# Query and key projections in 2x2 blocks of seven half-deep products, with the queries' rms division moved into the masking step

## The chip, the cores and the metric

The kernel runs on one core of a Trainium2 chip. [...] The metric is the device time of one execution in microseconds; lower is better. The kernel before took 1167.87 us (median of three runs, 1166.95 to 1168.11).

## The reference

Input x is 32 sequences of 32 tokens with 512 features, fp32 throughout. Four layers are added to it in turn:

```
x = x + mix(x)        # a 32x32 matrix per sequence, picked from 16
x = x + base(x) + lora(x)   # 512x512, and a rank-32 part picked from 5
x = x + adapt(x)      # a 512x512 matrix per sequence, picked from 8
x = x + attention(x)
```

The attention layer is the one that changes:

```
q = x @ Wq.T   # 32 heads of 128;  k, v = x @ Wk.T, x @ Wv.T: 8 heads of 128
q, k = rmsnorm(q) * q_norm_w, rmsnorm(k) * k_norm_w     # over the 128 of a head
q, k = rope(q, pos), rope(k, pos)                       # halves of a head turned by cos, sin
k_all, v_all = 512 rows of a paged cache (16 pages of 32), then the 32 new rows
scores = q . k_all / sqrt(128), masked where the cached row is past the sequence's length
out = softmax(scores) @ v_all, heads joined, @ Wo.T
```

Four query heads share one key head. There are 1024 tokens, so 8 tiles of 128.

## The kernel before, in words

**Stage 1** (0 to about 123 us) does the first three layers for the eight tiles t, software-pipelined, and turns each finished tile into `x3t(t)`: 512 features as 4 slices (KC) of 128 on the partitions, 128 tokens in the columns. The `adapt` matrices, 1 MB each and 32 of them, stream in on SyncE.

**The query and key stage** (123 to 401 us). The weights of q, k and v are 12 chunks (NCH) of 512 outputs, that is 4 heads: chunks 0 to 7 queries, 8 and 9 keys, 10 and 11 values. A chunk's weights are loaded by `load_qkv` (L303, 1 MB). For each chunk and tile `project` (L322) makes four matmuls (`project_part`, L307, L308) of 128x512, summed in one PSUM bank. Then, for queries and keys: `squares` on ScalarE (L335, from PSUM), `sums` on VectorE (L339), `roots` (L343), `inverses` (L347), `rotate`, `scales` (L366, one ScalarE multiplication per head) and `store_heads`. `rotate` forms product times cosine table (L351) and two halves of product times sine table (L356) on VectorE, straight from the PSUM bank, and adds them on GpSimd (L362). The norm weights lie in the tables `cw` and `sw`. `store_heads` transposes 32x32 blocks on VectorE (L375) and stores four transfers to DRAM (`q_d`, `k_d`; L384). `projected_evenly` (L402) writes out by hand the order of these steps on TensorE, VectorE and ScalarE, one tile behind; GpSimd and SyncE are not in that hand order. Values (chunks 10, 11) are only copied (L315) and stored to `v_d`. Chunk 0 and one tile of chunk 1 are done within stage 1. In this stage the pages of keys and values of the first two sequences are loaded (`load_pages`, `load_values`, the latter as indirect transfers on GpSimd, L246), and 20 of the 32 heads' output weights (`load_wo(0, ...)`, 16 transfers of 320 KB on SyncE, L692).

**Attention** (from 401 us) runs over 256 units (sequence b, key head g), written out by hand for all five engines. A unit n does: scores (two matmuls, L754, L755, into one pair of PSUM banks that all units share), then on VectorE the masking step L763: scores times -1/sqrt(128) plus the mask, with its minimum `low`; on ScalarE the exponential with its sum (L772); transposes and placements (L785, L797 ScalarE, L799 GpSimd, L801 VectorE); eight units later the products with the values (L825). The rest of TensorE's time carries the output projection (`share` and `finish`, L902) from unit 37 on, and in units 0 to 36 `fill`: one matmul of chunk 11 (values) at a time, 32 of them with five units left empty. Pages for sequence b+1 are loaded on SyncE in the first half of sequence b, 12 at its first unit and 4 at its fifth. The other 12 heads' output weights (`load_wo(1, ...)`, 192 KB each) follow from unit 37 on.

Two places of stage 1 matter for the prediction too: `angles` makes the tables, whose products run on GpSimd (L577 to L580), and `mixers` multiplies two SBUF tiles of 128x128 on VectorE (L463, then L470 adds the identity).

Of the kernel before, what the change touches and what calls it, by code (L numbers as in the profile page):

```python
# [12 lines left out]
F32 = mybir.dt.float32  # L13
# [7 lines left out]
P = 128  # L21
# [14 lines left out]
HALF = HQ // 2  # L36
QUAD = 4
AHEAD = 8
VS_BUFS = 4
# [18 lines left out]
def cond_resid_kernel(  # L58
# [29 lines left out]
    x_d = dram.tile([NT, P, HID], F32, name="x_d")  # L88

# [30 lines left out]
    eps_t = const.tile([P, 1], F32, name="eps_t")  # L120
    half_pi = const.tile([P, 1], F32, name="half_pi")
# [8 lines left out]
    def constant_values():  # L130
# [3 lines left out]
        nc.gpsimd.memset(eps_t, EPS)  # L134
        nc.gpsimd.memset(half_pi, HALF_PI)
# [63 lines left out]
    homes, kts, vts, vns, qts = {}, {}, {}, {}, {}  # L199
# [12 lines left out]
    def see_keys(b: int):  # L212

        nc.vector.tensor_scalar(
            mask, key_i, len_f[:, b : b + 1], -1.0e30, ALU.is_ge, ALU.mult
        )
# [4 lines left out]
    def load_queries(b: int, q: int):  # L221
# [4 lines left out]
        )  # L226

# [41 lines left out]
    ahead = pa.enter_context(ExitStack())  # L269
    wqps[0] = ahead.enter_context(tc.tile_pool(name="a_wq0", bufs=1))  # L270
    turn = ahead.enter_context(ExitStack())
    wp = turn.enter_context(tc.tile_pool(name="a_w", bufs=1))
    tp = turn.enter_context(tc.tile_pool(name="a_t", bufs=3))
# [38 lines left out]
    def store_values(ps, c: int, t: int):  # L312
        c0 = (c - (HQ + HK) // REP) * HID
        vs = vsp.tile([P, HID], F32, tag="vs", name=f"vs_{c}_{t}")
        copied = nc.scalar.copy(vs, ps)  # L315
        if (c, t) == (NCH - 2, 1):

            with tc.issue_after(copied.ins):
                nc.scalar.activation(warm, eps_t, AF.Exp)
        nc.scalar.dma_start(out=v_d[t * P : (t + 1) * P, c0 : c0 + HID], in_=vs)  # L320

    def project(c: int, t: int):  # L322
        ps = accumulator(f"qkv_{c}_{t}", c >= (HQ + HK) // REP)
        for k in range(KC):
            project_part(ps, c, t, k)
        if c >= (HQ + HK) // REP:
            store_values(ps, c, t)
            return None
        return SimpleNamespace(
            c=c, t=t, i=0 if c < HQ // REP else 1, ps=ps.rearrange("p (h d) -> p h d", h=REP)  # L330
        )

    def squares(u):
        u.sq = tp.tile([P, REP, D], F32, tag="sq", name=f"sq_{u.c}_{u.t}", bufs=2)
        nc.scalar.activation(u.sq, u.ps, AF.Square)  # L335

    def sums(u):
        u.ss = tp.tile([P, REP], F32, tag="ss", name=f"ss_{u.c}_{u.t}")
        nc.vector.tensor_reduce(u.ss, u.sq, AX.X, ALU.add)  # L339

    def roots(u):
        u.rms = tp.tile([P, REP], F32, tag="rms", name=f"rms_{u.c}_{u.t}")
        nc.scalar.activation(u.rms, u.ss, AF.Sqrt, bias=eps_t, scale=1.0 / D)  # L343

    def inverses(u):
# [760 lines left out]
```

## Time and profile before

| | us |
|---|---|
| median of three runs | 1167.87 |
| the profiled execution's own time | 1172.85 |
| its span, first to last instruction | 1170.8 |
| TensorE busy | 1157.2 |
| VectorE busy | 798.3 |
| ScalarE busy | 753.4 |
| GpSimd busy | 432.0 |
| query and key stage, TensorE's unbroken run of L308 | 278.1 (123.0 to 401.1) |

"Busy" of an engine is the time in which one of its instructions ran; TensorE's matmuls overlap, so the mean time of one (593 ns) is longer than its share of the busy time. A group's line gives the source line, engine, operation, output and inputs with their shapes, the count, the busy time and the mean of one in ns, and behind the last bar the idle time of that engine just before them with what ended it. An fp32 matmul is recorded as two passes, so a count of matmuls is twice that of the program. A window's line gives each engine's busy time in a stretch of time, the granted TensorE clock (1.00 is full), the share of the transfer engines' time and GB/s. A timeline's line has the start, the time, and the instruction; "x2" means that two followed each other and are merged.

### The profile page before, as it was taken

The page shows a single profiled execution, that of the slowest core. Times are in us where ns is not written, and L with a number is a line of the kernel's source. Part 1 is how long each engine was busy: PE and PEld are TensorE (multiplying, and loading weights), DVE is VectorE, ACT ScalarE, POOL GpSimd, SP SyncE. Part 2 cuts the span into 40 slices and gives each one's busy share as a digit, 9 for nine tenths or more (in the row PEclk, how much of TensorE's full clock was granted, in tenths as well). Part 3 has the DMA queues.
Part 4 walks back from the last instruction along what each step waited for, and adds up shares of the span by engine and source line. Part 5 has one row for each costly group of instructions (what it writes and reads, how often), then busy time and mean ns, then how long its engine had stood idle before and what let it go on. Part 6 is the DMA issues. An engine that isn't in the chain of part 4 may idle for free.

```text
span 1170.8 us, 19718 instructions
## 1 busy us (share of the span) xinstructions
PE 1157.2 (99%) x5512; PEld 747.1 (64%) x5512; DVE 798.3 (68%) x1782; ACT 753.4 (64%) x1652; POOL 432.0 (37%) x571
## 2 busy tenths in 40 slices
PE   8999999999999999999999999999999999999998
PEld 5444444444444467776777777777777777777766
DVE  2524488777777168767777777777777877877861
ACT  1223376656565378877777777877877877777750
POOL 3301544333333055344433443443444344344410
PEclk9999999999999999999999999999999999999999
DMA  8997866565545647789676677767766766775710
GB/s 320 388 390 289 325 152 161 156 159 153 139 117 129 201 137 236 261 259 261 208 257 213 208 230 242 224 208 237 241 203 221 252 223 198 254 243 186 230 41 10
DMA packets 180879, 250.64 MB, mean 214 GB/s; under 512 B 21250, under 2 KB 140674, under 8 KB 175010
## 3 DMA queue, kind: packets, MB, share of 16 engines
q1 hardware_dynamic: 156802, 163.52, 45.2%
q0 software_dynamic: 19216, 69.35, 17.8%
q10 hardware_dynamic: 4752, 16.52, 4.1%
q8 instruction: 45, 0.74, 0.3%
q14 instruction: 64, 0.52, 0.1%
HBM read 219.94 MB, written 29.36 MB: 213 GB/s over the span
## 4 chain that ended last, share of the span: by engine, by line
PE 87%; DVE 4%; ACT 2%; SPq 2%; DMA 2%; issue 2%; POOL 0%; ACTq 0%; DVEq 0%; POOLq 0%
PE qkv L308 28%; PE o_ps L825 16%; PE f_ps L902 14%; PE s_ps L754 10%; PE s_ps L755 8%; PE adapt L540 2%; PE base L515 2%; DMA kt<-in_k_cache_dram 2%; ACT placed L797 1%; PE o_ps L845 1%; DVE pr L763 1%; PE pn_ps L812 1%; PE low_ps L496 1%; SPq L194 1%; ACT pr L772 1%
## 5 line engine op out<-in xcount | busy, mean ns | idle before, releaser
L797 ACT COPY placed<-turned 32x512 f32<-32x512 f32 x539 | 332.1, 616 | 32.6 <-DVE turned L785 22.9
L825 PEld LDWEIGHTS o_ps<-vt,placed 128*128 128x128 f32 x2048 | 267.9, 192 | 119.9 <-issue 95.6
L308 PE MATMUL qkv<-wq,x3t 128*128 128x512 f32 x768 | 336.7, 593 | 0.3 <-ACT vs L315 0.3
L763 DVE CUSTOM_DVE_ANT_0 pr<-s_ps,mask 128x544 f32<-128x544 f32 x256 | 185.6, 725 | 169.0 <-PE s_ps L755 153.0
L772 ACT ACTIVATE pr<-pr,low 128x544 f32<-128x544 f32 x256 | 191.6, 749 | 138.0 <-DVE low L763 93.3
L825 PE MATMUL o_ps<-vt,placed 128*128 128x128 f32 x2048 | 271.7, 276 | 2.7 <-DVE ot L882 1.3
L308 PEld LDWEIGHTS qkv<-wq,x3t 128*128 128x128 f32 x768 | 145.1, 190 | 171.4 <-issue 167.5
L799 POOL COPY placed<-turned 32x512 f32<-32x512 f32 x268 | 163.6, 610 | 228.4 <-DVE turned L785 174.6
L902 PE MATMUL f_ps<-wo,ot 128*128 128x512 f32 x480 | 242.1, 596 | 0.3
L362 POOL TENSOR_TENSOR ra<-ra,rs 128x512 f32<-128x512 f32 x80 | 101.6, 1270 | 210.5 <-DVE rs L356 189.1
L785 DVE STREAM_TRANSPOSE turned<-pr 128x512 f32<-128x512 f32 x256 | 178.6, 698 | 0.1
L754 PE MATMUL s_ps<-kt,qt 128*128 128x288 f32 x512 | 174.0, 421 | 0.6 <-issue 0.5
L755 PE MATMUL s_ps<-kt,qt 128*128 128x256 f32 x512 | 152.5, 379 | 2.0 <-DMA kt<-in_k_cache_dram 2.0
L246 POOL DMA_INDIRECT vt<-in_v_cache_dram,v_idx x128 | 127.3, 995 | 36.0 <-issue 25.0
L366 ACT ACTIVATE ra<-ra,rinv 128x128 f32<-128x128 f32 x320 | 101.8, 390 | 29.0 <-POOL ra L362 17.3
L755 PEld LDWEIGHTS s_ps<-kt,qt 128*128 128x128 f32 x512 | 97.1, 190 | 29.4 <-issue 2.8
L902 PEld LDWEIGHTS f_ps<-wo,ot 128*128 128x128 f32 x480 | 85.9, 191 | 28.2 <-issue 13.9
L801 DVE COPY placed<-turned 32x512 f32<-32x512 f32 x217 | 96.7, 445 | 5.5
L808 POOL COPY pq<-pr 128x128 f32<-128x128 f32 x64 | 18.5, 289 | 184.8 <-ACT pr L772 164.2
L754 PEld LDWEIGHTS s_ps<-kt,qt 128*128 128x128 f32 x512 | 77.5, 191 | 13.3 <-DVE low L763 5.9
L351 DVE TENSOR_TENSOR ra<-qkv,cw 128x512 f32<-128x512 f32 x80 | 54.9, 687 | 35.5 <-ACT sq L335 35.5
L335 ACT ACTIVATE sq<-qkv 128x512 f32<-128x512 f32 x80 | 47.3, 591 | 46.5 <-PE qkv L308 44.8
(99 smaller groups left out, 749.4 us busy)
## 6 DMA issues: line engine op xcount, KB each, us to landing
kt<-in_k_cache_dram SPq DMA_DIRECT2D x512, 128.0 KB
wa<-in_w_adapt_dram SPq DMA_DIRECT2D x32, 1024.0 KB
q_d<-st SPq DMA_DIRECT2D x256, 64.0 KB
qt<-q_d SPq DMA_DIRECT2D x64, 256.0 KB
wq<-in_w_qkv_dram ACTq DMA_DIRECT2D x10, 1024.0 KB
wo<-in_w_o_dram SPq DMA_DIRECT2D x16, 320.0 KB
k_d<-st SPq DMA_DIRECT2D x64, 64.0 KB
v_d<-vs ACTq DMA_DIRECT2D x16, 256.0 KB
```

The lines of the kernel that those rows point to most:

```text
L246: nc.gpsimd.indirect_dma_start(out=vts[b][:, c, :], out_offset=None, in_=v_cache, in_offset=bass.IndirectOffsetOnAxis(ap=v_idx[:, at : at ...
L308: nc.tensor.matmul(ps, x3t(t)[:, k, :], ws[c][:, k, :], start=(k == 0), stop=(k == KC - 1))
L366: nc.scalar.activation(u.a[:, h, :], u.a[:, h, :], AF.Copy, scale=u.rinv[:, h : h + 1])
L754: nc.tensor.matmul(ps[:, first:L], q, kt4[:, :N_LOW, g, :], start=True, stop=True)
L755: nc.tensor.matmul(ps[:, L : first + LT], q, kt4[:, N_LOW:, g, :], start=True, stop=True)
L763: nc.vector.tensor_tensor_reduce(pr, ps[:, first : first + LT], mask, -SCALE, 3.0e38, ALU.add, ALU.min, low)
L772: nc.scalar.activation(pr, pr, AF.Exp, bias=low, scale=-1.0, accum_out=dens[quad][:, u : u + 1])
L785: nc.vector.transpose(part, pr)
L797: nc.scalar.copy(dst, src)
L799: nc.gpsimd.tensor_copy(dst, src)
L825: nc.tensor.matmul(po, pt[:, c, :], vt[:, c, g * D : (g + 1) * D], start=(c == 0 and q == 0), stop=(c == L // P - 1 and q == 1),)
L902: nc.tensor.matmul(pfs[t][:, :HID], ots[t, h // HALF][:, h % HALF, :], wo(h), start=(h == 0), stop=(h == (HQ if t < NT - 1 else HALF) - 1),)
```

## The change: seven products for eight, and the division moved

Two neighbouring chunks (a pair) and two neighbouring tiles make a 2x2 block of outputs, and the 512 features are cut into two halves of 256. Four output tiles would take eight products of half depth (two matmuls each); the change makes seven by Strassen's scheme in Winograd's form. That needs sums of the inputs and of the results:

- `token_sums` (GpSimd, stage 1): four sums of 128x256 for each of the four pairs of tiles.
- `weight_sum` (four for each of the five pairs of chunks, 128x1024 each): on VectorE (V) or GpSimd (G), within the stage for all pairs but the first.
- `product`: two matmuls; products 6 and 7 are added onto product 1 in its bank, and 3 onto 5, after ScalarE has copied the bank out (`out_of`).
- `formed`: each output tile is the sum of a copied part and a PSUM bank (three on VectorE) or of two copied parts (one on GpSimd). It now lies in SBUF. `by_cos` (VectorE) and `by_sin` (one half on VectorE, one on GpSimd) read it there; `rotated` adds on GpSimd as before.

The queries are no longer scaled on ScalarE. Their squares are summed per head by ScalarE (`accum_out`), the inverse roots are stored to DRAM (`r_d`), loaded for each sequence, and used as the scalar per row of the masking step; the sign goes into the queries' norm weights and the mask. Keys are scaled as before.

Values of chunk 10 take chunk 0's place in stage 1; two tiles of chunk 11 are projected at the end of the stage, and the other six remain as fills in units 0 to 36. `load_wo(0, ...)` moves to attention units 1 to 16. The whole stage has a hand-written order by slots, one slot a product, GpSimd included: `at(slot, ...)` puts a step behind the product of that slot.

```diff
-VS_BUFS = 4
+VS_BUFS = 2
...
-            mask, key_i, len_f[:, b : b + 1], -1.0e30, ALU.is_ge, ALU.mult
+            mask, key_i, len_f[:, b : b + 1], 1.0e30, ALU.is_ge, ALU.mult
...
+    def load_inverses(b: int):
+        rqs[b] = const.tile([P, 2, QUAD], F32, tag="rq", name=f"rq_{b}", bufs=2)
+        nc.sync.dma_start(out=rqs[b], in_=r_d[b].rearrange("r s h g -> (r s) h g"))
...
+    PAIRS = [(HQ // REP, HQ // REP + 1)] + [(c, c + 1) for c in range(0, HQ // REP, 2)]
...
+        b11, b12, b21, b22 = w[:, 0, :KH], w[:, 1, :KH], w[:, 0, KH:], w[:, 1, KH:]
+        out, a, b = {
+            1: (d[:, 0], b12, b11),
+            2: (d[:, 1], b22, d[:, 0]),
+            3: (b12, b22, b12),
+            4: (d[:, 2], b21, d[:, 1]),
+        }[n]
+        eng.tensor_tensor(out, a, b, ALU.subtract)
...
+        nc.gpsimd.tensor_tensor(s1, b[:, :KH], b[:, KH:], ALU.add)
+        nc.gpsimd.tensor_tensor(s2, s1, a[:, :KH], ALU.subtract)
+        nc.gpsimd.tensor_tensor(s3, a[:, :KH], b[:, :KH], ALU.subtract)
+        nc.gpsimd.tensor_tensor(s4, a[:, KH:], s2, ALU.subtract)
...
+        for k in range(KH):
+            nc.tensor.matmul(
+                ps,
+                of[:, k],
+                by[:, k],
+                start=(not more and k == 0),
+                stop=(k == KH - 1),
+                skip_group_check=more,
+            )
...
+    def formed(u, a, b, eng):
+        u.x = tp.tile([P, REP, D], F32, tag="x", name=f"x_{u.c}_{u.t}", bufs=5)
+        eng.tensor_tensor(u.x.rearrange("p h d -> p (h d)"), a, b, ALU.add)
+
+    def by_cos(u):
+        u.a = tp.tile([P, REP, D], F32, tag="ra", name=f"ra_{u.c}_{u.t}", bufs=5)
         nc.vector.tensor_tensor(
-            u.a, u.ps, cw[:, u.i, u.t, :].unsqueeze(1).to_broadcast([P, REP, D]), ALU.mult
+            u.a, u.x, cw[:, u.i, u.t, :].unsqueeze(1).to_broadcast([P, REP, D]), ALU.mult
...
+        eng.tensor_tensor(
+            u.s[:, :, to],
+            u.x[:, :, of],
+            sw[:, u.i, u.t, to].unsqueeze(1).to_broadcast([P, REP, H2]),
+            ALU.mult,
+        )
...
+        for h in hs:
+            junk = tp.tile([P, D], F32, tag="sq", name=f"sq_{u.c}_{u.t}_{h}", bufs=2)
+            nc.scalar.activation(
+                junk, u.x[:, h, :], AF.Square,
+                accum_out=roots_of[half, u.t][:, h, g : g + 1],
+            )
...
+    M_ORDER = (1, 5, 2, 6, 3, 7, 4)
...
+        at(g + 1, lambda: out_of("r1", b.X, "r", 2))
+        at(g + 2, lambda: out_of("r5", b.Z, "r5", 1))
+        at(g + 3, lambda: formed(u11, b.r1, b.Y, V))
+        at(g + 3, by_cos, u11)
+        at(g + 4, lambda: out_of("r2", b.X, "r", 2))
+        at(g + 4, by_sin, u11, 0, V)
+        at(g + 4, by_sin, u11, 1, G)
+        at(g + 5, lambda: formed(u12, b.r2, b.Z, V))
+        at(g + 5, by_cos, u12)
+        at(g + 5, rotated, u11)
+        at(g + 6, lambda: out_of("r3", b.X, "r", 2))
+        at(g + 6, by_sin, u12, 0, V)
+        at(g + 6, by_sin, u12, 1, G)
+        at(g + 7, lambda: formed(u21, b.r3, b.W, V))
+        at(g + 7, by_cos, u21)
+        at(g + 7, lambda: formed(u22, b.r3, b.r5, G))
+        at(g + 8, rotated, u12)
+        at(g + 8, by_sin, u21, 0, V)
+        at(g + 8, by_cos, u22)
+        at(g + 9, by_sin, u21, 1, G)
+        at(g + 9, by_sin, u22, 0, V)
+        at(g + 9, by_sin, u22, 1, G)
+        at(g + 10, rotated, u21)
+        at(g + 11, rotated, u22)
...
+    BLOCKS = [(0, 0), (1, 0), (0, 1), (0, 2), (1, 1), (0, 3), (1, 2), (1, 3)]
+    BLOCKS += [(i, p) for i in range(2, len(PAIRS)) for p in range(NP)]
+    for n, i in ((8, 3), (12, 4)):
+        at(7 * n + 2, load_pair, i)
+    at(7 * 6 + 2, load_pair, 2)
+    for g, i in ((7 * 7, 2), (7 * 9, 3), (7 * 13, 4)):
+        at(g, weight_sum, i, 1, V)
+        at(g + 2, weight_sum, i, 2, V)
+        at(g + 4, weight_sum, i, 3, G)
+        at(g + 11, weight_sum, i, 4, G) if i > 2 else at(g + 5, weight_sum, i, 4, V)
+    at(4, weight_sum, 1, 1, V)
+    at(5, weight_sum, 1, 3, G)
+    at(6, weight_sum, 1, 2, V)
+    at(8, weight_sum, 1, 4, V)
+    at(7 * 3 + 1, load_pages, 0)
+    at(7 * 4 + 1, load_values, 0)
...
-            pr, ps[:, first : first + LT], mask, -SCALE, 3.0e38, ALU.add, ALU.min, low
+            pr,
+            ps[:, first : first + LT],
+            mask,
+            rqs[b][:, g // QUAD, u : u + 1],
...
-    fills = [(t, k) for t in range(NT) for k in range(KC)]
-    EMPTY = (10, 13, 21, 29, 34)
+    fills = [(t, k) for t in range(2, NT) for k in range(KC)]
+    FILLED = 37
...
+            if 1 <= n <= REP * REP:
+                load_wo(0, *divmod(n - 1, REP))
```

In this notation u11 and u12 are the first and second chunk of the pair at the first tile, u21 and u22 at the second; g is a block's first slot. Transposes (`store_heads`) of a query block stand at slots g+6 (u11), g+9 (u12), g+11 (u21) and g+13 (u22). For queries the squares take the place of a key block's squares, sums, roots, inverses and scales.

## Prediction

> **What bounds the kernel now.** I read the page's busy shares first, then the costliest groups, then the windows of the query and key stage, then the waits.
>
> ```profile
> span 1170.8 us, 19718 instructions
> PE 1157.2 (99%) x5512; PEld 747.1 (64%) x5512; DVE 798.3 (68%) x1782; ACT 753.4 (64%) x1652; POOL 432.0 (37%) x571
> L308 PE MATMUL qkv<-wq,x3t 128*128 128x512 f32 x768 | 336.7, 593 | 0.3 <-ACT vs L315 0.3
> L362 POOL TENSOR_TENSOR ra<-ra,rs 128x512 f32<-128x512 f32 x80 | 101.6, 1270 | 210.5 <-DVE rs L356 189.1
> ```
> ```profile
> core 0: us, PE busy (x) PEld busy (x) DVE busy (x) ACT busy (x) POOL busy (x), PEclk, DMA share, GB/s
> 160.00:200.00 40.00, 40.00 (x94) 17.67 (x93) 35.92 (x83) 28.44 (x84) 17.82 (x14) 1.00 0.62 159
> 240.00:280.00 40.00, 40.00 (x95) 17.76 (x94) 29.67 (x68) 24.09 (x70) 13.95 (x11) 1.00 0.65 178
> ```
>
> TensorE bounds this stage without a gap: 40.00 of every 40 us at clock 1.00, and 0.3 us idle before all of L308. Its chain shows 278.1 us of nothing else, from 123.0 to 401.1 us. The chain's "x8" pieces of L308 last 3.43 us, so an fp32 matmul (two recorded passes) takes 0.859 us and a tile of four 3.43 us. GpSimd has the most room (14 of 40 us).
>
> **What is removed.** Ten chunks x 8 tiles x 4 = 320 matmuls become 5 pairs x 4 x 7 products x 2 = 280. 40 x 0.859 = **34.4 us** less TensorE. A block of four tiles falls from 13.74 to 7 x 1.718 = 12.03 us. If TensorE stayed the bound, that would be all. So the question is what else fits into 12.03 us.
>
> **What is added per block.** *ScalarE* (queries): four copies out of PSUM at 0.58 (L315) and sixteen squares of 128x128 with a sum. The trace has no such square; its parts are 0.318 (L366's busy time / 320) and 0.186 for reading a sum (L772), so 0.32 to 0.576 (0.390 + 0.186) each. I take 0.50, as both rows overlap in part in the timeline: 16 x 0.50 + 2.3 = 10.3 us; even the upper end gives 11.5. It fits. Keys: four squares 0.58, roots 0.30, scales 1.28, copies: 10.9 us.
>
> *VectorE* (queries), by the pitch in the timeline (512 wide 0.60, 256 wide 0.335, transpose 0.62): three sums 1.8, four cos products 2.4, four half sin products 1.34, four transposes 2.5 = 8.0 us. Keys add four reduces and reciprocals: 4 x (0.60 + 0.14) = 2.96.
>
> *GpSimd*: five 512-wide operations at a pitch of 1.23 (L577 to L579 back to back) and four halves. A half on GpSimd is not in the trace: between 0.64 and 1.27; I take 0.69, near the lower end, since its copies of 128 and 512 columns (0.289, 0.610) leave about 0.18 fixed, (1.27 - 0.18)/2 + 0.18 less the overlap. Sum 8.9 us.
>
> Each fits alone. **But not together.** Before, the rotation on VectorE read its products from PSUM; now cos and sin products read the copied tile and the table both from SBUF, while GpSimd works from SBUF too. One place in the trace has that pair:
>
> ```profile
> 44.53 2.58 POOL L580 TENSOR_TENSOR sw<-sn,nw 128x512 f32<-128x512 f32 x2 [21.51 <-ACT sn L566]
> ```
> ```profile
> 44.80 1.16 DVE L463 TENSOR_TENSOR md<-mg,quarter 128x128 f32<-128x128 f32 x1
> 46.00 1.25 DVE L470 TENSOR_TENSOR md<-md,ident 128x128 f32<-128x128 f32 x1
> 47.18 0.68 DVE L547 TENSOR_TENSOR xs<-xs,adapt 128x512 f32<-128x512 f32 x1
> 55.17 0.28 DVE L463 TENSOR_TENSOR md<-mg,quarter 128x128 f32<-128x128 f32 x1
> ```
>
> The first column is the start, the second the time. L463 takes 0.28 us elsewhere, and 1.16 beside GpSimd's two: it ends at 45.96, 0.14 after the first GpSimd operation (44.53 + 1.29). L470 then ends 0.14 after the second. L547, with one input in PSUM, is not delayed (0.68). So a two-SBUF-input operation of VectorE waits for GpSimd's whole instruction. GpSimd lost only about 0.05 us (1.32 for 1.27), though VectorE took 0.13 in between: some 0.09 of its start lies beside it.
>
> I laid out one query block by hand with this rule, each engine in its program order, PSUM and copies ready, and 0.17 us from VectorE's end to GpSimd's start (241.81 to 241.98, L356 to L362). VectorE: form u12 to 0.60; cos u12 waits for 1.38, to 1.93; transpose u22 (of the block before) to 2.57; sin u12 waits for 3.78, to 4.07; transpose u11 4.69; form u21 5.29; cos u21 waits for 5.47, to 6.02; sin u21 6.62 to 6.91; cos u22 7.51 to 8.06; sin u22 9.24 to 9.53; transpose u12 10.15; form u11 10.75; cos u11 10.93 to 11.48; transpose u21 12.10; sin u11 12.43. GpSimd: add u11 0.15 to 1.38; sin u12 1.93 to 2.55; form u22 3.78; add u12 4.24 to 5.47; sin u21 6.02 to 6.62; sin u22 6.91 to 7.51; add u21 8.06 to 9.24; add u22 9.70 to 10.93; sin u11 11.48 to 12.08; then add u11 again at 12.60. The cycle is 12.43 us; with the one tie (2.55) given to VectorE, 12.3. I take **12.3**: just over TensorE's 12.03.
>
> [...]
>
> **Extras on the same two engines**, within the stage: weight sums (128x1024), ten on VectorE at 1.15 (from 0.414 for 256 and 0.687 for 512: 1.07 ns a column) = 11.5; six on GpSimd at 2.3 (twice 1.27 less the fixed part) = 13.8; eight gathers of values at 1.0 (L246) = 8.0, now queued between GpSimd's additions, which VectorE's transposes wait for; the keys' 2.96 x 4 = 11.8. Together 45.1. The lower bound is 0 (all beside waits of the other engine), the upper 45.1; I take three quarters, 33.8, since the hand layout leaves neither engine a hole longer than 0.5 us. TensorE has four plus two PSUM banks of slack, some 5 us, and then waits with them.
>
> **Stage end.** First sum after one value tile and three products behind 123.0: 131.6. 131.6 + 20 x 12.3 + 33.8 = 411.4; the two value tiles (6.9 us of TensorE) lie beside the last block's additions and transposes. Scores began at 401.1: **+10.3 us**.
>
> **Attention.** Eight matmuls of values leave it (6.9 us), but three of them from the first eight units, where the chain already shows waits for VectorE, ScalarE and GpSimd; 5 x 0.86 = **-4.3**. The 16 output-weight loads (5.2 MB) move to units 1 to 16 on SyncE, ahead of later key pages, new values and queries; before, 3.1 MB on that queue stood beside 2.0 us of TensorE waiting for key pages, bounded above by the chain's three key pieces (17.6 us). By size 2.0 x 5.2/3.1 = 3.4; I take **+3** with the 32 loads of inverses. Masking with a scalar per row instead of a constant: 0 to 0.06 us x 256 (tensor-scalar 128x8, L554 0.227 beside L609 0.169); hidden, as VectorE waits 153 us for scores; uncovered it is 15 us. The inverses' stores and loads land a third of a batch before use: 0. Pair loads (2.1 MB) come five products (8.6 us) before their first sum; at 230 GB/s (390 seen, 160 in use) 9.1 us: 0 to 3 us each, taken as 0. Stage 1 loads 1 MB more; its loads wait 42.5 us for TensorE, so 0.
>
> Profiled: 1172.85 + 10.3 - 4.3 + 3 = 1181.9. The median stands 4.98 below the profiled run: **1177**.
>
> **Rivals.** *TensorE stays the bound* (0.12): the engines' lag stays under 5 us. 1172.85 - 34.4 + 2.6 (the three hidden fills) + 3 = 1144, median 1139. For it: no engine's own sum exceeds 12.03; against: the two rows at 44.80 and 46.00. *The shared port costs, but less* (0.25): the chain keeps TensorE's pace and half the extras hide. This ends faster: 131.6 + 240.6 + 22.5 = 394.7, so -6.4 - 4.3 + 3, median 1160. It decides when stage overhead beyond TensorE's 12.03 per block falls below 32 us. *Longer chain* (0.12): 12.9 a block, all extras, 2 us waited for each of three pair loads: 440.7, +39.6 - 4.3 + 3, median 1206. *Between* (0.08): within 0.2% of 1168, about what can be told from no change. The forecast, 1170 to 1186, has 0.43. So faster 0.37, same 0.08, slower 0.55. The range 1146 to 1198 leaves out the first rival and half the third.
>
> **What would show it.** Right: cos and sin products of 512 and 256 columns at 1.0 us and more on VectorE instead of 0.69 and 0.41, ending just behind a GpSimd instruction; TensorE with gaps in the stage that end with ScalarE's copies or VectorE's sums, above all around weight sums and gathers; scores at 405 to 420 us. Wrong: TensorE gapless at 12.03 us a block, scores near 375; or the delay sits in attention, in waits for key pages behind output weights.

## The result and the profile after

The changed kernel takes **1230.55 us** (median of four runs, 1229.06 to 1232.01) beside 1167.99 for the kernel before on the same chip: a ratio of 1.0535, 95% interval 1.0516 to 1.0553. The forecast was 1177, and its range ended at 1198. The profiled execution took 1232.01 us, its span 1230.2.

Two instants divide both spans: the first and the last masking instruction, that is the first and last start in the view of the tile `pr` on VectorE (the three numbers ahead are the shortest, median and longest in ns). Before:

```profile
L763 DVE CUSTOM_DVE_ANT_0 pr<-s_ps,mask x256: 724/725/727, 402.1 to 1123.1; 128x544 f32<-128x544 f32 x128
```

After:

```profile
L975 DVE CUSTOM_DVE_ANT_0 pr<-s_ps,mask,rq x256: 774/784/789, 437.1 to 1182.8; 128x544 f32<-128x544 f32 x128
```

| us | start to first masking | first to last masking | behind | span |
|---|---|---|---|---|
| before | 402.1 | 721.0 | 47.7 | 1170.8 |
| after | 437.1 | 745.7 | 47.4 | 1230.2 |
| difference | +35.0 | +24.7 | -0.3 | +59.4 |

So two places have to be explained, the query and key stage with its end (+35.0) and the attention loop (+24.7). The page of after begins (PE is TensorE, PEld its weight loads, DVE VectorE, ACT ScalarE, POOL GpSimd; SP, further down, is SyncE):

```profile
span 1230.2 us, 19727 instructions
PE 1142.3 (93%) x5432; PEld 736.6 (60%) x5432; DVE 872.4 (71%) x1664; ACT 743.3 (60%) x1876; POOL 588.5 (48%) x695
```

TensorE has 80 fewer recorded passes, 40 matmuls, as the change says, yet 93% instead of 99% of a longer span. Four windows of after show where it stands:

```profile
core 0: us, PE busy (x) PEld busy (x) DVE busy (x) ACT busy (x) POOL busy (x), PEclk, DMA share, GB/s
240.00:280.00 40.00, 33.52 (x75) 14.11 (x74) 39.69 (x49) 21.57 (x112) 37.70 (x28) 0.98 0.45 125
400.00:420.00 20.00, 19.79 (x47) 8.43 (x45) 19.83 (x30) 10.32 (x53) 18.63 (x16) 1.00 0.41 92
420.00:440.00 20.00, 2.01 (x5) 1.58 (x6) 4.71 (x9) 4.99 (x19) 2.60 (x2) 0.62 0.46 105
480.00:500.00 20.00, 8.90 (x31) 6.27 (x32) 4.41 (x10) 3.33 (x7) 1.97 (x3) 0.59 1.02 250
```

**In the stage** (first line) VectorE and GpSimd are both full, 39.69 and 37.70 of 40 us, and TensorE loses 6.5. The groups say what they are full of (mean ns behind the busy time):

```profile
L422 POOL TENSOR_TENSOR ra<-ra,rs 128x512 f32<-128x512 f32 x80 | 114.5, 1433 | 21.3 <-DVE rs L414 20.7
L414 POOL TENSOR_TENSOR rs<-x,sw 128x256 f32<-128x256 f32 x80 | 86.3, 1089 | 16.2 <-DVE x L402 15.9
L406 DVE TENSOR_TENSOR ra<-x,cw 128x512 f32<-128x512 f32 x80 | 89.4, 1117 | 2.1
```

A cosine product (L406) takes 0.677 us at its shortest and 1.117 on average; a half sine product on GpSimd 0.713 and 1.089. In all TensorE waits 26.2 us in 13 stalls that end with a copy of ScalarE, and ScalarE is late because the squares that stand ahead of its copies wait 60.2 us for VectorE's sums (and 24.4 for GpSimd's):

```profile
L435 ACT ACTIVATE sq<-x 128x128 f32<-128x128 f32 x256 | 76.0, 300 | 85.5 <-DVE x L402 60.2
```

Another 5.9 us go at 132 us, where ScalarE sits on the issue of chunk 11's weights.

**At the stage's end** (third line of the windows) nobody works. The timelines of VectorE and TensorE there (start, time, instruction, and in brackets the idle time before it and what ended it):

```profile
425.05 0.71 DVE L477 STREAM_TRANSPOSE st<-ra 128x512 f32<-128x512 f32 x1 [2.81 <-DMA q_d<-st]
...
426.97 0.71 DVE L477 STREAM_TRANSPOSE st<-ra 128x512 f32<-128x512 f32 x1 [0.95 <-DMA q_d<-st]
437.05 0.78 DVE L975 CUSTOM_DVE_ANT_0 pr<-s_ps,mask,rq 128x544 f32<-128x544 f32 x1 [9.38 <-DMA q_d<-st]
```
```profile
412.76 7.03 PE L317 MATMUL qkv<-wq,x3t 128*128 128x512 f32 x16
437.99 1.30 PE L966 MATMUL s_ps<-kt,qt 128*128 128x288 f32 x2 [18.20 <-DVE low L975]
```

The last product of the last block ends at 412.8, the two value tiles at 419.8, and GpSimd's last addition, which starts at 421.76 and takes 1.26 us, at 423.0. The transposes lag to 427.7, since each needs one of three buffers `st` that a store must empty first; SyncE issues 24 stores of inverses and 36 of queries back to back from 403 to 435 us. Then the first masking waits 9.4 us more for the last query stores (the bracket of its line). What it reads was there: TensorE made the first unit's scores at 302.9 us, and the load of its inverses was issued at 398.0. So the likely cause, which no run tests alone, is that its output tile takes over memory of `st`. TensorE idles 18.2 us, and its clock falls (1.30 us instead of 0.65 for the pass of L966).

**In attention** TensorE waits for transfers, which before took it 2.0 us there:

```profile
PE s_ps L966 <- DMA wo<-in_w_o_dram: 12.4, 2, 8.9
PE s_ps L967 <- DMA kt<-in_k_cache_dram: 7.3, 3, 5.8
```

(us in total, times, longest; window 440 to 660.) These waits stand at units 16 and 24, the first of a sequence, and the granted clock is 0.59 in the window of the longest. From 640 us on the two kernels run alike.

### The profile page after: what moved, and what is told of

It is laid out like the page before. It is cut to its first block, busy times and chain, and to the rows that moved or that the text cites. A ratio compares the mean times of both kernels' runs of the same rounds, so it can differ in the third digit from the quotient of the medians.

```text
span 1230.2 us, 19727 instructions
## 1 busy us (share of the span) xinstructions
PE 1142.3 (93%) x5432; PEld 736.6 (60%) x5432; DVE 872.4 (71%) x1664; ACT 743.3 (60%) x1876; POOL 588.5 (48%) x695
## 3 DMA queue, kind: packets, MB, share of 16 engines
q0 software_dynamic: 19216, 69.35, 16.8%
## 5 line engine op out<-in xcount | busy, mean ns | idle before, releaser
L975 DVE CUSTOM_DVE_ANT_0 pr<-s_ps,mask,rq 128x544 f32<-128x544 f32 x256 | 200.7, 784 | 170.0 <-PE s_ps L967 154.0
L966 PE MATMUL s_ps<-kt,qt 128*128 128x288 f32 x512 | 175.4, 424 | 35.2 <-DVE low L975 20.0
L967 PE MATMUL s_ps<-kt,qt 128*128 128x256 f32 x512 | 154.0, 383 | 7.3 <-DMA kt<-in_k_cache_dram 7.3
L435 ACT ACTIVATE sq<-x 128x128 f32<-128x128 f32 x256 | 76.0, 300 | 85.5 <-DVE x L402 60.2
L422 POOL TENSOR_TENSOR ra<-ra,rs 128x512 f32<-128x512 f32 x80 | 114.5, 1433 | 21.3 <-DVE rs L414 20.7
L967 PEld LDWEIGHTS s_ps<-kt,qt 128*128 128x128 f32 x512 | 97.7, 192 | 35.8 <-issue 9.2
L966 PEld LDWEIGHTS s_ps<-kt,qt 128*128 128x128 f32 x512 | 78.3, 192 | 50.3 <-issue 35.2
L386 PE MATMUL m<-t_pair,x_sums 128*128 128x512 f32 x160 | 79.4, 620 | 21.7 <-ACT r L516 15.9
L414 POOL TENSOR_TENSOR rs<-x,sw 128x256 f32<-128x256 f32 x80 | 86.3, 1089 | 16.2 <-DVE x L402 15.9
L406 DVE TENSOR_TENSOR ra<-x,cw 128x512 f32<-128x512 f32 x80 | 89.4, 1117 | 2.1
L386 PE MATMUL m<-w_pair,x_sums 128*128 128x512 f32 x160 | 77.4, 623 | 10.4 <-ACT r L516 10.4
```

The source lines that it names most:

```text
L386: nc.tensor.matmul(ps, of[:, k], by[:, k], start=(not more and k == 0), stop=(k == KH - 1), skip_group_check=more,)
L422: nc.gpsimd.tensor_tensor(u.a, u.a, u.s, ALU.add)
L966: nc.tensor.matmul(ps[:, first:L], q, kt4[:, :N_LOW, g, :], start=True, stop=True)
L967: nc.tensor.matmul(ps[:, L : first + LT], q, kt4[:, N_LOW:, g, :], start=True, stop=True)
L975: nc.vector.tensor_tensor_reduce(pr, ps[:, first : first + LT], mask, rqs[b][:, g // QUAD, u : u + 1], 3.0e38, ALU.add, ALU.min, low,)
```

## The experiments

My theory after this reading was that three losses add up: the waits of VectorE beside GpSimd where both inputs lie in SBUF (the prediction and e1's expectation call it a port that the two share; that it is one, no run shows), the missing cover at the stage's end, and the output weights beside the key pages. Rivals: SyncE's queue (SyncE's and ScalarE's transfers share eight semaphores in turn, and in the trace of after 1265 of SyncE's 1276 wait for their own semaphore ahead of their issue, so in the program a long transfer holds all behind it), the 64 stores of inverses, the scalar per row, or one single cause behind all. All runs (no run is called e16), with what the profile of each shows, in us:

| run | median us | ratio to before (95%) | first masking | first to last |
|---|---|---|---|---|
| e1 | 1221.32 | 1.0437 (1.0401-1.0472) | 420.3 | 751.1 |
| e2 | 1231.72 | 1.0524 (1.0502-1.0546) | 433.6 | 746.4 |
| e3 | 1226.27 | 1.0476 (1.0458-1.0493) | 435.6 | 739.2 |
| e4 (before + edit) | 1197.08 | 1.0230 (1.0201-1.0259) | 401.3 | 745.9 |
| e5 (before + edit) | 1175.68 | 1.0045 (1.0028-1.0062) | 401.4 | 724.6 |
| e6 | 1238.91 | 1.0574 (1.0537-1.0611) | 437.0 | 752.2 |
| e7 | 1246.87 | 1.0643 (1.0625-1.0660) | 440.8 | 760.3 |
| e8 | 1240.64 | 1.0600 (1.0583-1.0618) | 437.4 | 750.3 |
| e9 | 1251.68 | 1.0723 (1.0702-1.0743) | 436.3 | 765.6 |
| e10 | 1227.26 | 1.0517 (1.0494-1.0540) | 440.9 | 736.4 |
| e11 | 1256.85 | 1.0783 (1.0741-1.0825) | 463.0 | 745.0 |
| e12 | 1221.59 | 1.0460 (1.0441-1.0479) | 411.3 | 760.4 |
| e13 (before + edit) | 1169.64 | 1.0000 (0.9990-1.0009) | 401.8 | 717.5 |
| e14 | 1228.85 | 1.0492 (1.0468-1.0516) | 435.7 | 749.9 |
| e15 | 1205.73 | 1.0305 (1.0288-1.0322) | 411.7 | 744.9 |
| e17 | 1189.27 | 1.0176 (1.0159-1.0193) | 411.6 | 727.4 |
| e18 | 1220.38 | 1.0430 (1.0396-1.0465) | 434.7 | 735.8 |
| e19 | 1194.11 | 1.0218 (1.0189-1.0246) | 415.4 | 728.7 |

Loop times (the last column) have to be compared with some care: the profiled run of before, whose loop took 721.0, is 4.9 us above its median, while e13, whose ratio is 1.0000, has 717.5. So what a run loses there against before may be up to 3.5 us more than the column says.

### The stage: VectorE's waits beside GpSimd

**e1**, the cosine table of the queries in PSUM:

```diff
+    cq = ps_s.tile([P, 2 * L], F32, tag="s", name="cq").rearrange("p (t d) -> p t d", d=D)
...
-            u.a, u.x, cw[:, u.i, u.t, :].unsqueeze(1).to_broadcast([P, REP, D]), ALU.mult
+            u.a,
+            u.x,
+            (cq[:, u.t, :] if u.q else cw[:, 1, u.t, :]).unsqueeze(1).to_broadcast([P, REP, D]),
+            ALU.mult,
```

> The queries' cosine table is copied once into the two PSUM banks that the scores use later, and the cos products of the queries read it there; nothing else changes. Theory A (VectorE's operations with two SBUF inputs wait for GpSimd's whole instruction, and this sets the stage): the 64 query cos products fall from about 1.1 us to 0.69, the stage's block end (412.8 us) moves to 395 to 405, the whole to 1210 to 1222. Rival B (the stage is set by ScalarE's copies and the transfer queues, the port only fills idle time): cos products fall too, but the stage end stays within 3 us and the whole at 1228 to 1232. Rival C (the waits move to the sin products and weight sums, which still have two SBUF inputs): cos products 0.69, sin products on VectorE rise above 0.83, whole 1222 to 1229.

The products with one input in PSUM no longer wait: in the view of their output tile they have a spread of 18 ns, and those of the keys, left as they were, one of 1008.

```profile
L406 DVE TENSOR_TENSOR ra<-x,cq x64: 672/686/690, 156.2 to 398.7; 128x512 f32<-128x512 f32 x64
L406 DVE TENSOR_TENSOR ra<-x,cw x16: 679/740/1687, 138.3 to 216.4; 128x512 f32<-128x512 f32 x16
```

The first masking comes 16.8 us earlier, and the ratio falls from 1.0535 to 1.0437. So the wait goes with the second input in SBUF, and this one operation costs 17 us of the stage. Attention gives 5.4 back.

**e11**, the addition on the other engine:

```diff
-        nc.gpsimd.tensor_tensor(u.a, u.a, u.s, ALU.add)
+        nc.vector.tensor_tensor(u.a, u.a, u.s, ALU.add)
```

> The changed kernel with the addition that ends the rotation on VectorE instead of GpSimd. Theory (VectorE waits in the stage for GpSimd's whole instructions, the 80 additions of 1.43 us above all): VectorE's own 8.0 + 2.4 us a block and GpSimd's remaining 3.8 fit into TensorE's 12.03, first masking 418 to 428 instead of 437, time 1212 to 1222 us. Rival (the two engines' sum decides, whoever adds): first masking 434 to 440 and 1228 to 1236 us.

A clear miss of both ranges: first masking 26 us later. GpSimd falls to 143 of the 300 us from 120 to 420 us, but VectorE takes on 80 additions of 1.04 us, and TensorE waits 40.4 us for the copies instead of 26.2. From 420 to 440 us VectorE is full (19.86 of 20 us) and GpSimd half empty (8.39), so here VectorE's own queue sets the pace, and the run doesn't separate that from the waits beside GpSimd. The rival had the side right, but the two engines' sum doesn't decide either: it fell (VectorE 273 and GpSimd 143 of the 300 us, before the edit 267 and 257), and the stage grew. Moving an operation's second input to PSUM helped (e1); handing this one to the engine with less room didn't.

### The stage's end

**e2**, 16 stores of inverses instead of 64 (`r_d` laid out as the tile is):

```diff
-        for j in range(BT):
-            nc.sync.dma_start(
-                out=r_d[t * BT + j, :, :, half, :].rearrange("r s g -> s r g"),
-                in_=root[j * S : (j + 1) * S],
-            )
+        nc.sync.dma_start(out=r_d[t, :, :, half, :], in_=root)
```

> The inverse roots are stored in 16 transfers of a whole tile instead of 64 of a quarter, in another layout of the scratch tensor. Theory A (SyncE's queue is full at the end of the stage: 64 stores at 0.47 us are 30 us of it, and the first masking waits for the last store of queries because its tile takes their memory): the first masking moves from 437.1 to 427 to 431 us, the whole falls by 6 to 12, to 1218 to 1225. Rival B (the first masking waits for something else, such as the inverses themselves): within 2 us of 1230.5.

First masking 3.4 us earlier, the ratio (1.0524) not distinguishable from after's. The theory missed its ranges; the time meets the rival's. The stores' number is a small part; the wait for the last query stores stays (8.4 us), so it isn't the inverses that the first masking waits for, as the rival guessed.

**e8**, the second sequence's pages spread out:

```diff
+    for n in range(NPP):
+        at(7 * 16 + 3 + 2 * n, load_page, 1, n)
```

> The changed kernel with the second sequence's 16 key pages issued one every second product (slots 115 to 145) instead of in one burst at slot 114. Theory (the burst of 14 us holds back the query stores behind it, and VectorE's transposes with them): VectorE's waits of 2.7 and 4.3 us at 372 to 383 us go, the first masking comes 4 to 8 us earlier than 437, time 1222 to 1227 us. Rival (the end of the stage is set by the transposes and the last stores alone): first masking at 436 to 439, 1229 to 1232 us.

First masking 437.4: the rival's place, but in the ratio (1.0600 beside 1.0535) slower than after and outside both ranges, by 4.6 us in attention (750.3 for 745.7). Why isn't shown: TensorE's waits from 440 to 660 us sum up to only 1.3 us more than in after.

**e10**, more cover:

```diff
-        for t in range(2):
+        for t in range(6):
             project(NCH - 1, t)
...
-    fills = [(t, k) for t in range(2, NT) for k in range(KC)]
+    fills = [(t, k) for t in range(6, NT) for k in range(KC)]
```

> The changed kernel with six value tiles at the end of the query and key stage instead of two, and 8 instead of 24 matmuls of values left as fills in units 0 to 36. Theory (TensorE's 18.2 us before the first masked scores are cover that is missing while the last transposes and their stores finish): four tiles more, 4 x 3.43 = 13.7 us, go into that hole, first masking stays at 436 to 439, time 1216 to 1222 us. Rival (units 0 to 36 without fills wait for the other engines instead): 1227 to 1233 us.

The hole shrinks from 18.2 to 8.6 us and attention by 9.3, but the first masking comes 3.8 later, and the ratio, 1.0517, is not distinguishable from after's: of 13.7 us next to nothing is left. In the first units TensorE is not the bound (16.43 of 20 us from 440 to 460 in after), so work taken out of them gains little; and 8.6 us of idling drop the clock as 18.2 do (0.60 from 440 to 460 us, and 1.30 us for the first passes of L966 behind them).

### The output weights in attention

**e4**, the kernel before with nothing but this move:

```diff
-                if 3 <= c < 3 + REP and t % 2 == 1:
-                    load_wo(0, c - 3, t // 2)
...
+            if 1 <= n <= REP * REP:
+                load_wo(0, *divmod(n - 1, REP))
```

> The kernel before, with one part of the change alone: the 16 loads of 20 heads' output weights move from the query and key stage to attention units 1 to 16, on SyncE. Theory A (the move itself costs some 20 us): 1180 to 1190. Rival B (the move is harmless where SyncE comes to it without a backlog, and costs only behind the late stores of the changed stage): 1167 to 1173. The prediction's term was +3.

The move alone makes the kernel before 26 us slower, 24.9 of it between first and last masking. Attention lost about as much in the changed kernel (24.7), where the row scalar and the fewer fills are in the sum too. Three windows of it, at unit 16:

```profile
core 0: us, PE busy (x) PEld busy (x) DVE busy (x) ACT busy (x) POOL busy (x), PEclk, DMA share, GB/s
440.00:445.00 5.00, 0.00 (x0) 0.00 (x0) 0.00 (x0) 0.00 (x0) 3.96 (x5) 0.78 1.03 201
450.00:455.00 5.00, 0.00 (x0) 0.00 (x0) 0.00 (x0) 0.00 (x0) 0.00 (x0) 0.50 1.05 320
455.00:460.00 5.00, 4.72 (x13) 3.50 (x14) 2.19 (x5) 1.97 (x4) 0.00 (x0) 0.51 1.07 197
```

TensorE, VectorE and ScalarE stand in the first two, the transfer engines are full, and where the output weights (packets of 2 KB to 32 partitions) fill them they move about 200 GB/s. SyncE's issues just before, and what TensorE waits for:

```profile
437.24 1.86 SPq L692 DMA_DIRECT2D wo<-in_w_o_dram  x4
439.20 0.38 SPq L224 DMA_DIRECT2D qt<-q_d  x1
439.76 2.47 SPq L194 DMA_DIRECT2D kt<-in_k_cache_dram  x4
445.30 6.36 SPq L692 DMA_DIRECT2D wo<-in_w_o_dram  x4
```
```profile
448.14 1.30 PE L752 MATMUL s_ps<-kt,qt 128*128 128x288 f32 x2 [9.52 <-DMA qt<-q_d]
455.28 1.19 PE L753 MATMUL s_ps<-kt,qt 128*128 128x256 f32 x2 [5.84 <-DMA kt<-in_k_cache_dram]
```

Half of the weights, 2.6 MB, are issued from 437 to 452 us, around the queries and the last pages that unit 16 needs. These queries are issued at 439.2, behind four of the weights, and the scores start at 448.1. So it is their landing that is late, behind weights that fill the transfer engines. At 200 GB/s the whole 5.2 MB take 26 us of the transfer engines. An average doesn't show the loss, though: in before, units 0 to 15 lie in this window (columns as above),

```profile
400.00:440.00 40.00, 39.36 (x182) 25.86 (x181) 21.59 (x50) 27.48 (x59) 17.79 (x31) 1.00 0.45 142
```

which leaves room for 0.55 x 40 = 22 us, 4 short of the 26, and the loss is 25. What counts is how the weights crowd with the transfers that a unit needs at once.

**e13**, the same with a fifth of the bytes:

```diff
+        n = 1 if i == 0 else w.shape[1]
+        nc.sync.dma_start(out=w[:, :n], in_=w_o4[r, k][:, g0 : g0 + n, :])
```

> The kernel before with the 16 output-weight loads moved to units 1 to 16, as in e4, but each brings one head of five (64 KB instead of 320; the other 16 heads' weights are left out and zeros stand in their place). Theory of bytes (the transfer engines lack the time for 5.2 MB there): a fifth of the loss of 26 us is left, 1170 to 1177 us. Rival, theory of places (each transfer takes one of the queue's eight places in flight, whatever its size): the loss stays, 1190 to 1198 us.

```profile
L764 DVE CUSTOM_DVE_ANT_0 pr<-s_ps,mask x256: 724/725/727, 401.8 to 1119.3; 128x544 f32<-128x544 f32 x128
```

Ratio 1.0000, and attention no longer than before: not even the fifth of the loss that the theory left. So the sixteen transfers as such cost nothing; their size does. Whether 320 KB each cost as time of the transfer engines or as time for which they hold the queue, this run doesn't separate, as a fifth of the bytes shortens both.

**e3**, the loads on GpSimd's queue:

```diff
-        nc.sync.dma_start(out=w, in_=w_o4[r, k][:, g0 : g0 + w.shape[1], :])
+        (nc.gpsimd if i == 0 else nc.sync).dma_start(out=w, in_=w_o4[r, k][:, g0 : g0 + w.shape[1], :])
```

> The 16 output-weight loads of units 1 to 16 are issued on GpSimd's queue instead of SyncE's; size, place and time stay. Theory A (the loads stand in SyncE's queue ahead of the key pages, and the eight transfers in flight fill with them): TensorE's waits of 8.9, 5.8 and 3.5 us at 476 to 519 us go, the whole falls by 15 to 24 to 1207 to 1216. Rival B (the transfer engines' bandwidth is short, whoever issues): the waits stay, 1225 to 1233. Rival C (GpSimd's queue is held instead, 16 x 1 us beside the placements): 1215 to 1225.

The waits at units 16 and 24 shrink from 19.0 to 6.0 us, with a new one of 3.2 us for ScalarE between them, and the ratio from 1.0535 to 1.0476. Part of the loss is therefore the order in SyncE's queue. Between first and last masking only 6.5 of the 24.7 us come back; what the loads cost on GpSimd's queue (rival C) wasn't measured apart, so the rest isn't assigned.

**e6** and **e7**, other units:

```diff
-            if 1 <= n <= REP * REP:
-                load_wo(0, *divmod(n - 1, REP))
+            if n % 2 == 1 and n < 2 * REP * REP:
+                load_wo(0, *divmod(n // 2, REP))
```

> The changed kernel with the 16 output-weight loads at units 1, 3, ... 31 instead of 1 to 16. Theory (too many bytes in the same queue and window as the key pages of the first sequences): the waits of 8.9 + 5.8 us at unit 16 and 3.5 + 0.7 at unit 24 shrink to a third, and with them the low clock behind them: 1212 to 1218 us. Rival (each such load costs the queue the same wherever it stands, so the waits only move on to the units behind 24): 1226 to 1231 us.

> The changed kernel with the 16 output-weight loads at units 21 to 36, as dense as before but where two batches' pages are ahead. Theory of density: the waits move to units 32 and 40 and stay about as long: 1224 to 1232 us. Rival (they hurt only because the first units follow the late stage end, with loads still queued from it): no wait over 2 us in these units, 1208 to 1214 us.

Both are slower than after (1.0574 and 1.0643). In e7 single waits of 14.0 us for a sequence's first scores and 9.9 for the output projection stand behind the loads, so none of the three places tried is quiet. That e6, with twice the time for the same bytes, has not less waiting but more (its longest is 10.4 us) I can't explain by bytes: an average of the room would have given it more.

**e9**, by 128 partitions:

```diff
+    def load_wide(g: int, k: int):
+        nc.sync.dma_start(out=wos[0][:, g * REP + k, :], in_=w_o4[:, k, :, g, :])
```

> The changed kernel with the 20 heads' output weights loaded as 20 transfers of 256 KB to all 128 partitions (units 1 to 20) instead of 16 of 320 KB to 32 partitions each (units 1 to 16). Theory (the transfers to 32 partitions are slow: the stretch where they alone filled the transfer engines moved about 200 GB/s, key pages 350 to 410): 5.2 MB then take 13 us of the transfer engines instead of 26, the waits at units 16 and 24 halve, 1208 to 1218 us. Rival (bytes and places in the queue decide, not the shape): 1226 to 1234 us.

A miss in the other direction, and not a test of what it was meant for. The 350 to 410 GB/s of its theory were mostly gathers of values, not key pages: from 484 to 488 us the changed kernel moved 391 GB/s, and the gathers took 79.5% of the transfer engines' time. Behind the pages the transfer engines are a quarter busy while everything waits (a window, columns as above):

```profile
490.00:493.00 3.00, 0.00 (x0) 0.00 (x0) 0.00 (x0) 0.00 (x0) 0.00 (x0) 0.50 0.26 97
```

Busy 0.26 of 16 is the time of some four engines, at 97 GB/s; from 488 to 494 us SyncE's transfers take 14.1% of the 16 engines' time and GpSimd's gathers 12.2%. Between 533 and 538 us each single microsecond shows 0.26 or 0.27 again. What holds the share there, no run shows. A load to 128 partitions that fills the transfer engines wasn't tried.

### Both losses undone

**e5**, the kernel before with the scalar from a tile of equal values:

```diff
-            pr, ps[:, first : first + LT], mask, -SCALE, 3.0e38, ALU.add, ALU.min, low
+            pr, ps[:, first : first + LT], mask, minus, 3.0e38, ALU.add, ALU.min, low
```

> The kernel before with one edit: the masking step's scalar comes from a tile of one value per partition instead of a constant. Masking instructions grow from 0.725 us by about 0.059, as in the changed kernel. Theory (hidden behind the wait for scores, 154 us in that group's idle time): 1168 to 1171 us, ratio within 0.998 to 1.002. Rival (the 256 instructions stand in the chain): 256 x 0.059 = 15 us more, ratio 1.013.

The instruction grows by 0.059 us (0.725 to 0.784), 15 us in 256 units. 3.6 us of it show between first and last masking (up to 7 against a before like e13's), 5.1 in the medians: between the two theories, mostly hidden.

**e14** and **e18** bring 16 heads' weights back into the stage, in the memory that the second sequence's pages had there. That sequence's 16 pages of keys (2.1 MB) and as much of values are loaded in the loop instead:

```diff
+    def open_weights():
+        last_pairs.close()
+        wop = ctx.enter_context(tc.tile_pool(name="b_wo", bufs=1, side="right"))
+        wos[0] = wop.tile([P, EARLY, HID], F32, name="wo_0")
+
+    at(7 * 16 + 2, open_weights)
+    for n in range(REP * REP):
+        at(7 * 16 + 2 + 3 * n // 2, load_wo, 0, *divmod(n, REP))
```

> The changed kernel with 16 of the 20 heads' output weights loaded in the query and key stage again (slots 114 to 136, in the memory that the second sequence's pages took there), the other four heads' in units 1 to 16 (64 KB each), and the second sequence's keys and values loaded in units 0 to 4 like those of all later ones. Theory (the 5.2 MB cost nothing beside the stage and 24 us beside the pages): attention, first to last masking, 720 to 728 us instead of 746, first masking 430 to 437, time 1203 to 1214 us. Rival (the second sequence's pages at unit 0 now come as late as the weights made others): 1224 to 1232 us.

Hardly a gain (1.0492 beside 1.0535), but the waits for pages at units 16 and 24 are down to 1.7 us and less. In their place stands one that I had made myself. TensorE's and GpSimd's timelines of e14:

```profile
482.48 1.86 PE L1047 MATMUL o_ps<-vt,placed 128*128 128x128 f32 x7 [15.71 <-POOL placed L1021]
```
```profile
461.21 1.25 POOL L1021 COPY placed<-turned 32x512 f32<-32x512 f32 x2 [3.93 <-DMA vt<-in_v_cache_dram,v_idx]
462.73 0.97 POOL L255 DMA_INDIRECT vt<-in_v_cache_dram,v_idx  x1 [0.27 <-POOL placed L1021]
467.41 1.25 POOL L1021 COPY placed<-turned 32x512 f32<-32x512 f32 x2 [3.71 <-DMA vt<-in_v_cache_dram,v_idx]
```

The second sequence's gathers now lie between GpSimd's copies, and each copy waits for the gather ahead of it. e18 issues the four gathers at unit 0:

```diff
+                if n == 0:
+                    load_values(1)
```

> e14 with the same edit: the changed kernel with 16 heads' output weights in the stage again and no gathers between GpSimd's copies. Theory (the moved weights cost the changed kernel what they cost alone, about 24 us, and e14 hid it behind 15.7 us of GpSimd's waits): first to last masking 722 to 732 us, time 1209 to 1219 us. Rival: 1225 to 1232 us.

1.0430 instead of 1.0535: 2.4 us less to the first masking and 9.9 less in attention (735.8 us), a little less than the theory's range wanted. Of the 24.7 us 14.8 are left in the loop, 3.6 of them the row scalar, 6.7 two waits at unit 16, where the second batch of pages is late now; the clock is 0.81 from 480 to 500 us. About as many bytes as in after pass through the first units here, 4.2 MB of pages and values for 4.2 MB of weights, and cost less. So bytes alone don't set the loss; shape, moment and order count, and these runs don't part them.

**e12**, five repairs together: e1, e2, e10, chunk 11's weights issued 14 products later, and the load of e9.

> The changed kernel with five edits: queries' cosine table in PSUM, inverses stored by 16 transfers, six value tiles at the stage's end, chunk 11's weights issued 14 products later on ScalarE, output weights by 128 partitions. Theory (each mends another loss): -12 - 13 - 5 - 12 from 1230 is 1188, 1183 to 1200 us. Rival (they all wait for the same stage end, so the gains overlap): 1203 to 1215 us. A third: the cosine table in PSUM alone is what counts, 1215 to 1222 us.

First masking 411.3, 25.8 us earlier; but e9's load took 14.7 back in attention (one wait of 19.5 us). Its time lies in the third range, not for that reason. **e15** is e12 with e14's placement in its stead, **e17** has e18's gathers as well, **e19** moves four of the heads into units 1 to 16 again:

```diff
-    EARLY = 16
+    EARLY = 12
...
-        at(7 * 16 + 2 + 3 * n // 2, load_wo, 0, *divmod(n, REP))
+        at(7 * 16 + 2 + 2 * n, load_wo, 0, *divmod(n, REP))
```

> e14 with the four edits of e12 that belong to the stage: cosine table in PSUM, inverses stored by 16 transfers, six value tiles at the stage's end, chunk 11's weights issued later. Theory (the losses of the stage and of the weights add up): first masking 408 to 414 as in e12, attention 710 to 718, 47 behind it: 1167 to 1180 us. Rival (the stage's end, now with 4.2 MB of weights beside it, moves out again): first masking 420 to 428, 1182 to 1195 us.

> e15 with the second sequence's four value gathers at unit 0 instead of units 8 to 11, where GpSimd's copies stood between them and waited 14.4 us. Theory (TensorE's one wait of 15.2 us for GpSimd at 459 us is that): it goes, 1188 to 1194 us. Rival (the gathers at unit 0 hold back the second sequence's key pages, so units 8 on wait for those): 1200 to 1208 us.

> e17 with 12 heads' output weights in the stage instead of 16, spread over slots 114 to 144, and 8 heads' (128 KB a load, 2.1 MB) in units 1 to 16. Theory (the query stores at the stage's end stand behind the weights, TensorE's 10.4 us before the first masking among it, and units 1 to 16 have room for 2 MB): first masking 405 to 410 instead of 411.7, 1182 to 1189 us. Rival (2 MB in units 1 to 16 is already too much): waits at units 16 and 24 again, 1192 to 1200 us.

e15 had its first masking where the theory put it (411.7) and missed both ranges of the time: the wait of e14 stood in it too, 15.2 us. e17 removes it, as the theory had it, and is the fastest version of the change, 1189.27 us:

```profile
L984 DVE CUSTOM_DVE_ANT_0 pr<-s_ps,mask,rq x256: 774/784/786, 411.6 to 1139.0; 128x544 f32<-128x544 f32 x128
```

Its stage still ends 9.5 us later than before's, and attention is 6.4 longer; a ratio of 1.0176 is left (1.0159 to 1.0193). So the repairs together undo two thirds of the difference, and no version that I tried beats the kernel before. In e17 TensorE waits 11.5 us in the stage and 10.6 for the first masking, and the clock is 0.59 from 420 to 440 us. e19 gained nothing at the stage's end (415.4), and its time, 1194.11, lies in the rival's range. Its 2.1 MB in units 1 to 16 bring waits for key pages back, most of them at units 16 and 24 (8.1 us in all, where e17 has 2.1), yet cost the loop only 1.3 us more than e17's 1.05 MB.

## Why the prediction failed, step by step

- **The sign**: slower, as forecast with 0.55, but 62.6 us instead of 9. Most of that stands in two places where the sum had nothing and +3, so the right sign is in good part luck.
- **TensorE's saving** (34.4 us): right in the count, 40 matmuls. None of it reached the end.
- **What fits**: ScalarE, right; a square with the reading of its sum takes 0.297 + 0.187 us, 0.50 was taken. GpSimd's half product 0.713 undisturbed, 0.69 was taken.
- **The block's cycle of 12.3 us by the two rows at 44.80 and 46.00**: not contradicted. Late in the stage, where nothing else disturbs, the same cosine product of successive blocks starts at 404.44 and 416.54, 12.10 us apart. TensorE's own pace is 12.03, and it has hardly a gap there (19.79 of 20), so the two engines need 12.10 at most. That VectorE's products wait beside GpSimd, as the two rows said, e1 shows by laying the table in PSUM (672 to 690 ns instead of up to 1.69 us).
- **Extras, three quarters of 45.1 (33.8)**: too low. The 411.4 of the forecast is where VectorE and GpSimd end the last block. TensorE's last product ends near it, at 412.8, by chance; GpSimd's last addition ends at 423.0, 11.6 us later than forecast. Of these 6.5 lie ahead of the first sum (138.1 for 131.6), most of them the 5.9 us behind the issue of chunk 11's weights, which no term had. The 20 blocks took 284.9 us for 279.8; by the forecast's own 12.3 that leaves 38.9 for the extras.
- **The stage's end**: wrong, the first of the two steps that failed. Scores stood in the sum at 411.4 as if nothing came behind the last block's additions. The value tiles do lie beside these additions (412.8 to 419.8), as the forecast says. But behind them come the last transposes (to 427.7), held by stores, and the last stores, for which the first masking waits (437.05): 14.0 us that the sum put at nothing. Forecast +10.3, measured +35.0; the 24.7 between are these 14.0 and the 11.6 above, less 0.95 by which masking stands behind the scores in before.
- **Fewer fills** (-4.3): not measured alone. e10, which takes 16 matmuls more out of the loop, shows 9.3 us less there.
- **Moved output weights, "I take +3"**: wrong, the other failed step and the term furthest off, 24.9 in e4. It was scaled by bytes from a place with 2.0 us of waits; e13 shows that 1.05 MB cost nothing in the same units, and e4 that 5.2 MB cost 24.9, so the cost isn't in proportion to the bytes. Even the upper bound of 17.6 was too low, as a bound from the waits of a lighter load is none.
- **Row scalar, hidden: 0**: 3.6 us (e5), within the bounds.
- **Inverses: 0**: 3.4 us at the stage's end (e2), hidden behind other waits in the time.

Up to the first masking the forecast misses 24.7 us, between first and last 26.0; another 3.5 is the profiled run of before, which stood 4.98 above its median where after's stands 1.46 above. Together 54.2, and the forecast missed by 53.6. Of the rivals, the longer chain named the right side with the wrong reason (12.9 us a block); the sentence on what would prove the text wrong, "waits for key pages behind output weights", named half of it.

What stays open: how much of the moved weights' loss is the transfer engines' time and how much the order in the queue, why spreading the weights over 32 units (e6) did not help, and some 4 us of e18's loop (14.8 less 3.6 and 6.7) that neither the scalar nor its long waits explain.

## What to carry to other kernels

A transfer that is moved has to be priced at its new place: its bytes by the rate that such a shape shows, and beside which transfers that a unit waits for it will stand. Neither a scaling by bytes from another place nor the average room in the loop gave the loss here. Where a stage's last instructions end in stores, follow them until the memory that they read is free, and ask which work stands beside them. And where VectorE's instructions with both inputs in SBUF stretch beside GpSimd's (here from 0.68 to 1.12 us on average), look first for an input that can lie in PSUM (e1); handing work from one engine to the other (e11) made it worse.

## What the runs showed of the hardware

- TensorE's granted clock was 0.50 in the windows inside and just behind its idle stretches (e4: 0.50 and 0.51 from 450 to 460 us), and the passes behind them took about twice their time: behind 18.2 us in the changed kernel the two of L966 1.30 us instead of 0.65, and already behind stalls of 3.45 and 0.74 us there, at 520.49 us, the two of L967 1.19 instead of 0.59. Each of these stalls so cost more than its length; the one of 18.2 us by some 2.0 us in its first six passes (an estimate from 1.30, 1.06 and 1.91 us instead of 0.65, 0.59 and 1.02).
- The output weights' transfers, 2 KB packets to 32 partitions, filled all transfer engines at 197 to 201 GB/s, where a window shared with gathers of values reached 320 (e4). No run here separates the partitions from the rest of the shape.
- VectorE's instructions with both inputs in SBUF stretched beside GpSimd's: cosine products took 0.677 to 1.686 us in the changed kernel. With one input in PSUM they keep their 0.69 us (e1: 672 to 690 ns). No run shows what the two engines share.
